# Filling the last block's gaps with the next gates, and re-ordering the entry of layer 3, in a four-layer graph network kernel

## The chip, the cores and the metric

The kernel runs on one core of one Trainium2 chip. The metric is device time in microseconds (us), the median of several runs; the profile comes from one further execution. The core's engines are named as in the profile: PE (matrix multiply), PEld (its weight loads), DVE (vector), ACT (scalar/activation), POOL (GpSimd) and SP (which here only issues DMAs). Each engine works through its own list of instructions in order and waits for others by semaphores.

## The reference, cut to what matters

Sixteen graphs (B) of 1024 nodes (N) with 256 features (D) pass through four pre-normalised layers. Each layer computes `h = relu(layernorm(x))` and adds its result to `x`. Layers 2 and 3 matter here:

```
# layer 2: a scan over nodes; node i reads rows that earlier nodes have already changed
norm_adjT = swapaxes(adj, 1, 2) / rowsum
def step(h, i):
    x = h_e[:, i];  x_par = norm_adjT[:, i] @ h
    r, z = sigmoid(split(x @ W_ioux.T + b_ioux + x_par @ W_iouh.T + b_iouh))
    hc = tanh(x @ W_coux.T + b_coux + (x_par * r) @ W_couh.T + b_couh)
    h[:, i] = z * x_par + (1 - z) * hc
# layer 3
agg = epsilon * h + adj @ h
y = silu(rmsnorm(agg @ W1 + b1)) ;  out = y @ W2 + b2
```

## The kernel before, in words

**Layers 0 and 1** come first and are not touched.

**Layer 2** cuts the 1024 nodes into NT = 8 blocks of 128 (`for t in range(NT)`) and each block into NS = 8 sub-slices of 16 nodes (`for s in range(NS)`), all sixteen graphs side by side. A sub-slice is computed in one or more steps (`SLICES`: one step of 16 nodes for s = 0 and 1, two of 8 for s = 2 to 6, and 8, 4, 4 with one repeated round for s = 7). A step is a chain across engines: `round_` multiplies by the recurrent weights (L1102, into `pr`, `pz`, `pc`), ACT applies sigmoid and tanh (L1146, L1153, L1163), DVE combines (L1147 to L1165), `turned` transposes the result (L1174) and ACT copies it out (L1177). Between two steps `x_change` (L1130) applies what the first step changed. At the end of a sub-slice PE computes `near`, the contribution to the next sub-slice (L1355), and DVE forms the next `x` from it (L1280).

A list `todo` holds independent PE work: contributions to later sub-slices (`far_tasks`, L1084, DVE adds them at L1087) and, while another block follows, the base sums of that next block (`base_tasks`, L935). `fill(weight)` takes pieces from `todo` and puts them between the steps of the chain; what a piece leaves to evict is queued in `late` and emitted by `evict()` at fixed places. The order of the instructions of PE, DVE, ACT and POOL in layer 2 is that of the program text.

The input side of the gates of the next sub-slice (`Gates`; three products of eight matmul records each, L1048, evicted by ACT for q = 0 at L1056 and by DVE for q = 1, 2 at L1053) is not in `todo`, except at s = 0. It is put in the two arms of a run-time branch (L1332): if a chain of dependent nodes is longer than the planned steps, `one_more` runs an extra round with the gates in its gaps; otherwise the Else arm runs the three gates one after the other. In the profiled execution the Else arm is what runs.

In the last block (t = 7) there is no next block, so `todo` holds only the far pieces. `early_3`, a generator, prepares layer 3 for graph 0 there: its first `next` issues the loads of `x`, of two adjacency quarters and of the layer-2 results; later calls normalise seven of the eight row tiles. For a tile DVE adds (L1413), takes statistics (L1415, L1416); then POOL takes the inverse root (L86) and ACT writes the relu (L1427). The kernel before calls it once per sub-slice, just ahead of the branch: three tiles per call, then the root and two diagonals, then all seven relus at once. Tile 7 exists only when layer 2 has ended and is done by `prepare(0)` in layer 3.

**Layer 3** works graph by graph. `sums` multiplies adjacency quarters by differences of `h` (a Strassen-like scheme of seven quarter products, L1522); the quarters go through six buffers `at`, filled by `fill(k)` (L1469), and five of the seven get epsilon added to their diagonals by POOL (`eps_of`, `diagonal`, L1389). `inner` multiplies by combinations of W1 (`ws`, L1568), `norm` and `outer` follow (L1639). At the entry POOL forms combinations of the weights (`ws` L1680 to L1683, `wt` L1687 to L1690), `row()` adds b2 to x (L1499), and `load(1)`, `prepare(1)` bring up graph 1. Only POOL follows the program text in layer 3; the order on the other engines, SP's issues among them, is made by a planner that also looks at costs and at the waits it is told (`issue_after`).

Entry order of POOL in the kernel before: root of tile 7, four `ws`, four `wt`, four pieces of `row`, then the diagonals of quarters 3, 4, 5, then that of quarter 6. SP: W1, tile 7's rows (`hn[0]` L1439), W2, b1, rms weight, b2, quarters 4 and 5, then x and the layer-2 rows of graph 1, then quarter 6.

Of the kernel before, what the change touches and what calls it, by code (L numbers as in the profile page):

```python
# [16 lines left out]
P = 128  # L17
# [25 lines left out]
def gnn_stack(ctx: ExitStack, tc: tile.TileContext, a: dict, out: bass.AP):  # L43
# [815 lines left out]
    def layer_2(shared, early):  # L859
        with ExitStack() as st:  # L860
# [172 lines left out]
            class Gates:  # L1033
# [9 lines left out]

                def gate(self, q):
                    pg = psum.tile([P, DC, G2 * GR], F32, name="pf", bufs=3)
                    for e in range(DC):
                        for c in range(DC):
                            nc.tensor.matmul(pg[:, e], wx[:, c, q * D + e * P : q * D + (e + 1) * P], self.hs[:, c],  # L1048
                                             start=c == 0, stop=c == DC - 1)

                    def out():
                        if q:
                            nc.vector.tensor_add(self.g[:, q], pg, bias[:, q][:, :, None].to_broadcast([P, DC, G2 * GR]))  # L1053
                        else:
                            for e in range(DC):
                                nc.scalar.activation(self.g[:, q, e], pg[:, e], AF.Identity, bias=bias[:, q, e : e + 1])  # L1056
                    return out
# [143 lines left out]
            with tc.manual_schedule(engines={mybir.EngineType.PE, mybir.EngineType.DVE, mybir.EngineType.Activation, mybir.EngineType.Pool}):  # L1201
# [19 lines left out]
                for t in range(NT):  # L1221
                    if t == NT - 1:
                        eye = next(early)
                    base_todo = deque()
                    if t + 1 < NT:
# [6 lines left out]
                    for s in range(NS):  # L1232
# [30 lines left out]
                        total = sum(cost for cost, _ in todo)  # L1263
                        spent = part = 0.0

                        def fill(weight):
                            nonlocal spent, part
                            part += weight
                            while todo and (part > 0.999 or spent + 0.5 * todo[0][0] < part * total):
                                cost, task = todo.pop(0)  # L1270
                                spent += cost
                                late.append(task() or (lambda: None))
# [22 lines left out]
                        for k, (i0, i1) in enumerate(steps):  # L1295
# [19 lines left out]
                            if k == 0:  # L1315
                                gx_now, gx = gx, gx_next
                                if s > 0 and sub_next:
                                    nc.gpsimd.tensor_copy(tick, rx[:, DC - 1].rearrange("p b i -> p (b i)")[:, :1] if K > 1
                                                          else rx[:, DC - 1, :1])
                                    gx = Gates(he if ahead[0] == t else he_next, ahead[1])  # L1320
                                    gx_ahead = Gates(he_next, 1) if s + 1 == NS else None
                            dh = h if last else work.tile([P, G2, D], F32, name="dh", bufs=1)
                            turned(change if twice else hT, rest_if(last, 0.5), dh)
                            if k == 0 and sub_next:
# [3 lines left out]
                                sub_next.own()  # L1328
                        if t == NT - 1 and s > 0:
                            next(early, None)  # L1330
                        in_arms = gx.tasks if gx and s > 0 else ()
                        with tc.If(n_more[0][s] > 0, preferred_fallthrough_block=False) as more_or_not:  # L1332
# [4 lines left out]
                        if in_arms:  # L1337
                            with more_or_not.Else():
                                for task in in_arms:
                                    late.append(task())  # L1340
                                    if len(late) > 1:
                                        late.pop(0)()
                                evict()
                        if gx:
                            gx.seed_r()
# [45 lines left out]
    def early_3(shared, pool, x, hn, at, h):  # L1391
# [20 lines left out]
        for t in range(n):  # L1412
# [3 lines left out]
            nc.vector.bn_aggr(mv[:, t], st)  # L1416
            if t % 3 == 2:
                yield
        rs = inv_sqrt(pool, mv[:, :, 1], LN_EPS, [P, n], "rs")
# [6 lines left out]
        for t in range(n):  # L1426
            nc.scalar.activation(h[0][:, t], x[0][:, t], AF.Relu, bias=shift[:, t : t + 1], scale=rs[:, t : t + 1])  # L1427
        yield

    def layer_3(shared, x, hn, at, h, eye):  # L1430
        with ExitStack() as st:
# [6 lines left out]
            eye, eye2 = eye  # L1438
            nc.sync.dma_start(hn[0][:, NT - 1], hs_d[NT - 1][0][:P])  # L1439
            w1 = wp.tile([P, DC, H], F32, name="w1")  # L1440
            nc.sync.dma_start(w1, a["W1"].rearrange("(c p) e -> p c e", p=P))
            w2 = wp.tile([P, HC, D], F32, name="w2")
            nc.sync.dma_start(w2, a["W2"].rearrange("(c p) e -> p c e", p=P))
            b1 = wp.tile([P, HC], F32, name="b1")
            rw = wp.tile([P, HC], F32, name="rw")
            with nc.allow_non_contiguous_dma(reason="weights, once"):
                nc.sync.dma_start(b1, a["b1"].rearrange("(c p) -> p c", p=P))
                nc.sync.dma_start(rw, a["rms_weight"].rearrange("(c p) -> p c", p=P))
            b2 = wp.tile([P, D], F32, name="b2")
            nc.sync.dma_start(b2, bcast_row(a["b2"], D))  # L1450

            NH = 512
            HH = HC // 2

            def load(b):
                if b:
                    x[b] = big.tile([P, NT, D], F32, name="x", bufs=3)
                    nc.sync.dma_start(x[b], rows(x2_d[b]))
                    hn[b] = shared.tile([P, NT, D], F32, name="hb")
                    nc.sync.dma_start(hn[b][:, : NT - 1], rows(hn_d[b])[:, : NT - 1])  # L1460
                    nc.sync.dma_start(hn[b][:, NT - 1], hs_d[NT - 1][b // GB][b % GB * P : (b % GB + 1) * P])

            NQ = len(ORDER)
# [10 lines left out]

            def prepare(b):

# [15 lines left out]
                nc.vector.scalar_tensor_tensor(shift, mv[:, part, 0], -1.0, rs, op0=ALU.mult, op1=ALU.mult)  # L1492
                for k, t in enumerate(tiles):
                    nc.scalar.activation(h[b][:, t], x[b][:, t], AF.Relu, bias=shift[:, k : k + 1], scale=rs[:, k : k + 1])  # L1494

# [15 lines left out]
            def sums(b, st, s4):  # L1511
# [29 lines left out]
                def third():  # L1541
# [9 lines left out]
                    product("s4", "b22", p7)  # L1551
                    nc.scalar.copy(tt[:, 2], p7)
                    nc.vector.tensor_sub(tt[:, 1], c11, p7)
                    nc.vector.tensor_sub(tt[:, 0], c22, tt[:, 1])
                    nc.vector.tensor_sub(tt[:, 3], c21, tt[:, 1])
                return (ag, tt), [first, second, third]

# [115 lines left out]

            load(0)
            for k in range(2, 6):
                fill(k)
            row = prepare(0)
            ws = wp.tile([P, 3, HH * P], F32, name="ws")
# [11 lines left out]
            nc.gpsimd.tensor_tensor(wt[:, 2], v21, wt[:, 1], ALU.subtract)  # L1690
            row()
            load(1)
            for k in range(2, 6):
                eps_of(k)
            st3, steps3 = differences(0)
            for step3 in steps3[:3]:
                step3()
            ags, parts = sums(0, st3, steps3[3])
            parts[0]()
            eps_of(NQ - 1)  # L1700
            parts[1]()
            parts[2]()
            prepare(1)()
            for k in range(4):
                eps_of(NQ + k)
            for b in range(B):
# [11 lines left out]
                if b + 1 < B:  # L1718
                    ags, parts = sums(b + 1, st3, s4)
                parts[0]()  # L1720
# [77 lines left out]
```

## Time and profile before

| | us |
|---|---|
| median of 3 runs | 4227.49 (4225.37 to 4234.3) |
| profiled execution, its own time | 4226.12 |
| its span, first to last instruction | 4224.4 |
| one block of layer 2, from near of s = 1 to the next block's (blocks 0 to 5) | about 202 |
| last block, near of s = 1 (2794.84) to the first product of layer 3 (2959.10) | 164.3 |
| first product of layer 3 to the first product of `inner` that follows the sums (3008.70) | 49.6 |
| one graph of layer 3, in the steady part | 76.2 |

Over the whole span PE is busy 95%, DVE 62%, ACT 39%, POOL 39%, and the granted clock of TensorE is 0.985. These are averages: a row of stretches (start and end in us, then busy us and instruction count of each engine, the granted clock as a share of full speed, the busy share of the DMA engines and GB/s) tells more. In the timeline rows the columns are start, duration (of a merged group), engine, line, operation, tiles, count, and in brackets the idle time before it and who ended it. Matmul records of one group overlap slightly in time; a gate product of four matmuls shows as eight records.

### The profile page before, as it was taken

To read this page: it belongs to the slowest core of one execution; us is meant where nothing else is said; L and a number is where in the kernel's file an instruction comes from. 1 tells how busy PE (TensorE), PEld (TensorE's weight loads), DVE (VectorE), ACT (ScalarE), POOL (GpSimd) and SP (SyncE) were. 2 spreads that over 40 slices of the span, in tenths; PEclk is the share of its full clock that TensorE was granted. 3 is DMA by queue.
4 is the path that set the end of the run, shared out by engine and by line. 5 is a ranking of instruction groups with operands and counts; after the bars stand their busy time and mean duration, and the time that the engine had idled before them with its cause. 6 is when DMAs were issued, how large, how long until landed. Compare 5 with 4: busy or idle time off the path is not lost. (4 is left out here: it accounts for less than half of the span.)

```text
span 4224.4 us, 56649 instructions
## 1 busy us (share of the span) xinstructions
PE 4018.3 (95%) x19307; PEld 2802.1 (66%) x19307; DVE 2614.6 (62%) x6218; ACT 1635.4 (39%) x4172; POOL 1646.5 (39%) x1740
## 2 busy tenths in 40 slices
PE   7999999998997999999999999998899999999998
PEld 3545455555555888888888888877365665756656
DVE  7888976577762444444444444453577877777776
ACT  3565565544543232232323232323233334333332
POOL 2232223434334324333333333332546355464552
PEclk9999999999998999999999999998899999999999
DMA  7576657988768454645464554421633434334320
GB/s 244 207 238 232 230 200 261 265 301 285 262 212 269 135 197 135 200 136 186 153 193 145 189 163 162 155 99 36 214 120 137 163 120 146 134 121 174 114 100 21
DMA packets 406704, 744.74 MB, mean 176 GB/s; under 512 B 75168, under 2 KB 325664, under 8 KB 365344
## 3 DMA queue, kind: packets, MB, share of 16 engines
q1 hardware_dynamic: 370976, 613.49, 42.5%
q0 software_dynamic: 26080, 109.21, 9.0%
q10 hardware_dynamic: 9216, 16.78, 1.1%
q8 instruction: 210, 3.44, 0.3%
q14 instruction: 222, 1.82, 0.1%
HBM read 538.85 MB, written 183.76 MB: 171 GB/s over the span
## 5 line engine op out<-in xcount | busy, mean ns | idle before, releaser
L86 POOL TENSOR_TENSOR rs<-rs_v,mhalf 128x8 f32<-128x8 f32 (+1 forms) x65 | 112.3, 1728 | 900.4 <-DVE rs_v L82 469.7
L935 PE MATMUL pf<-hb,ab 128*128 128x256 f32 x1568 | 415.2, 383 | 0.0
L1048 PE MATMUL pf<-hs,wx 128*128 128x256 f32 x1536 | 347.7, 383 | 13.0 <-POOL hs L1039 12.7
L1048 PEld LDWEIGHTS pf<-hs,wx 128*128 128x128 f32 x1536 | 293.5, 192 | 56.2 <-POOL hs L1039 13.8
L1348 POOL DMA_INDIRECT hs_d<-h,table x128 | 129.3, 1010 | 464.6 <-ACT gates L1056 404.3
L1576 POOL TENSOR_TENSOR ss<-ss,sq 128x512 f32<-128x512 f32 x224 | 299.2, 1351 | 23.8 <-ACT sq L1574 17.8
L935 PEld LDWEIGHTS pf<-hb,ab 128*128 128x128 f32 x1568 | 272.1, 191 | 37.3 <-issue 6.7
L1053 DVE TENSOR_TENSOR gates<-pf,bias 128x512 f32<-128x512 f32 x128 | 88.5, 692 | 288.3 <-PE pf L1048 248.4
L423 PE MATMUL pmm<-w,ag 128*128 128x256 f32 x1024 | 234.6, 387 | 20.4 <-DVE x L427 8.8
L1639 PEld LDWEIGHTS po<-w,hh 128*128 128x128 f32 x2048 | 237.9, 193 | 16.6 <-issue 11.0
L1639 PE MATMUL po<-w,hh 128*128 128x128 f32 x2048 | 242.1, 277 | 1.4 <-ACT hh L1622 0.7
L423 PEld LDWEIGHTS pmm<-w,ag 128*128 128x128 f32 x1024 | 196.1, 194 | 61.6 <-DVE x L427 12.6
L1574 ACT ACTIVATE sq<-hh 128x512 f32<-128x512 f32 x224 | 141.6, 632 | 197.7 <-POOL ss L1576 118.7
L1522 PE MATMUL ph<-bxt,hb 128*128 128x512 f32 x440 | 198.9, 598 | 4.1 <-ACT hb L1494 2.6
L1146 ACT ACTIVATE r<-pr 128x128 f32<-128x128 f32 (+2 forms) x256 | 57.9, 278 | 366.4 <-PE pr L1102 306.4
L1084 PE MATMUL pf<-bd,h 128*128 128x384 f32 (+4 forms) x512 | 185.1, 451 | 0.8 <-DVE bxt L1087 0.8
L1087 DVE TENSOR_TENSOR bxt<-bxt,pf 128x384 f32<-128x384 f32 (+4 forms) x256 | 128.0, 501 | 82.3 <-PE pf L1084 79.5
L1572 DVE SCALAR_TENSOR_TENSOR hh<-ph,b,u 128x512 f32<-128x512 f32 x192 | 141.5, 749 | 47.0 <-PE ph L1568 36.9
L1622 ACT ACTIVATE hh<-hh,rw 128x512 f32<-128x512 f32 x256 | 158.9, 711 | 24.1 <-DVE hh L1621 24.1
L345 ACT ACTIVATE pt<-x,m_neg 128x256 f32<-128x256 f32 x240 | 114.5, 477 | 109.0 <-DVE m_neg L340 102.7
L1621 DVE TENSOR_TENSOR hh<-hh,po 128x512 f32<-128x512 f32 x256 | 154.3, 679 | 2.9 <-PE po L1618 2.9
L1494 ACT ACTIVATE hb<-x,shift,rs 128x256 f32<-128x256 f32 x120 | 60.9, 591 | 239.6 <-DVE shift L1492 239.6
(371 smaller groups left out, 9283.3 us busy)
## 6 DMA issues: line engine op xcount, KB each, us to landing
at<-in_quarters SPq DMA_DIRECT2D x94, 1024.0 KB
t_d<-at SPq DMA_DIRECT2D x64, 1024.0 KB
ab<-in_columns SPq DMA_DIRECT2D x127, 512.0 KB
bxt<-t_d SPq DMA_DIRECT2D x42, 1024.0 KB
bxt<-in_quarters SPq DMA_DIRECT2D x34, 1024.0 KB
at<-at POOLq DMA_DIRECT2D x30, 1024.0 KB, 7.1
at<-t_d SPq DMA_DIRECT2D x22, 1024.0 KB
pc<-in_own ACTq DMA_DIRECT2D x64, 256.0 KB
```

The source lines that it names most:

```text
L423: nc.tensor.matmul(po[:, t - t0], ag[:, c, t * P : (t + 1) * P], w[:, c], start=c == 0, stop=c == DC - 1)
L935: nc.tensor.matmul(pb, ab[:, jts[k]], hb[:, jts[k]], start=k == 0, stop=k == len(jts) - 1)
L1048: nc.tensor.matmul(pg[:, e], wx[:, c, q * D + e * P : q * D + (e + 1) * P], self.hs[:, c], start=c == 0, stop=c == DC - 1)
L1084: nc.tensor.matmul(pf, h[:, g, c * P : (c + 1) * P], bd[:, g, b0 : b0 + n, S : S + far], start=True, stop=True)
L1348: nc.gpsimd.indirect_dma_start(out=hs_d[t][g][:, :], out_offset=row(1, g, t, s), in_=h[:, g], in_offset=None)
L1522: nc.tensor.matmul(pa, st[left][:, k], at[q % 6][:, k], start=onto is None and k == 0, stop=k == 3, skip_group_check=True)
L1572: behind3[:] = [nc.vector.scalar_tensor_tensor(hh[q][:, k], ph, b1[:, k : k + 1], u, op0=ALU.add, op1=ALU.add)]
L1574: nc.scalar.activation(sq, hh[q][:, k], AF.Square)
L1576: nc.gpsimd.tensor_tensor(ss[q], ss[q], sq, ALU.add)
L1621: nc.vector.tensor_mul(hh[q][:, k], hh[q][:, k], pr)
L1622: nc.scalar.activation(hh[q][:, k], hh[q][:, k], AF.Silu, scale=rw[:, k : k + 1])
L1639: nc.tensor.matmul(po[:, n], left[:, c, n * P : (n + 1) * P], right[:, c], start=onto is None and n == 0 and c == 0, stop=c == HH - 1, ski ...
```

## The change

Four things are done.

1. In the last block, for s = 1 to 6, two of the three next gates are appended to `todo` once `x` of the next sub-slice's gates can be read, so that `fill` places them between the steps; one stays in the arms. In every block the last gate's PSUM tile is now taken ahead of the branch, and its eviction is emitted after the branch (`out_of_arms`) and not in both arms.
2. `early_3` yields after every tile, in the statistics and in the relus, and is called from `fill` (so from `late`) for s > 1 in the last block, in place of one call per sub-slice for s > 0.
3. At the entry of layer 3 the fills and diagonals of quarters 2 to 5 come ahead of the weights, b2 ahead of W2, tile 7's rows behind W2; `row()` of graph 0 and `load(1)` come ahead of the `ws`/`wt` combinations on POOL.
4. The relus of graph 1 (`prepare(1)`) are told to be issued after the ACT copy `tt` at the end of graph 0's sums.

```diff
-                def gate(self, q):
-                    pg = psum.tile([P, DC, G2 * GR], F32, name="pf", bufs=3)
+                def gate(self, q, pg=None):
+                    if pg is None:
+                        pg = psum.tile([P, DC, G2 * GR], F32, name="pf", bufs=3)
...
-                    base_todo = deque()
+                    base_todo = None
...
+                        in_arms, out_of_arms = [], None
                         def fill(weight):
                             nonlocal spent, part
+                            if t == NT - 1 and s > 1:
+                                late.append(lambda: next(early, None))
                             part += weight
...
                                     gx = Gates(he if ahead[0] == t else he_next, ahead[1])
                                     gx_ahead = Gates(he_next, 1) if s + 1 == NS else None
+                                    n = 0 if base_todo is not None else 2
+                                    todo += [(1.72, task) for task in gx.tasks[:n]]
+                                    total += 1.72 * n
+                                    in_arms = gx.tasks[n:]
...
-                        if t == NT - 1 and s > 0:
-                            next(early, None)
-                        in_arms = gx.tasks if gx and s > 0 else ()
+                        if in_arms:
+                            pg = psum.tile([P, DC, G2 * GR], F32, name="pf", bufs=3)
+                            def last_gate():
+                                nonlocal out_of_arms
+                                out_of_arms = gx.gate(2, pg)
+                                return lambda: None
+                            in_arms = in_arms[:-1] + [last_gate]
                         with tc.If(n_more[0][s] > 0, ...) as more_or_not:
...
+                            out_of_arms()
                         if gx:
                             gx.seed_r()
...
             nc.vector.bn_aggr(mv[:, t], st)
-            if t % 3 == 2:
-                yield
+            yield
...
             nc.scalar.activation(h[0][:, t], x[0][:, t], AF.Relu, ...)
-        yield
+            yield
...
     def layer_3(shared, x, hn, at, h, eye):
...
-            nc.sync.dma_start(hn[0][:, NT - 1], hs_d[NT - 1][0][:P])
+            for k in range(2, 6):
+                fill(k)
+                eps_of(k)
             w1 = ...load W1
+            b2 = ...load b2
             w2 = ...load W2
+            nc.sync.dma_start(hn[0][:, NT - 1], hs_d[NT - 1][0][:P])
             b1, rw = ...load b1, rms_weight
-            b2 = ...load b2
...
-            def prepare(b):
+            def prepare(b, behind=None):
...
+                with tc.issue_after(behind) if behind is not None else ExitStack():
                     for k, t in enumerate(tiles):
                         nc.scalar.activation(h[b][:, t], ...)
...
-                    nc.scalar.copy(tt[:, 2], p7)
+                    got["tt"] = nc.scalar.copy(tt[:, 2], p7)
...
-            load(0)
-            for k in range(2, 6):
-                fill(k)
-            row = prepare(0)
+            prepare(0)()
+            load(1)
             ws = ...four POOL operations; wt = ...four POOL operations
-            row()
-            load(1)
-            for k in range(2, 6):
-                eps_of(k)
...
-            prepare(1)()
+            prepare(1, got["tt"].ins)()
```

In the instruction lists as built, SP now issues at the entry: W1, quarters 4 and 5, b2, W2, tile 7's rows, b1, rms weight, quarter 6, then x and the layer-2 rows of graph 1. POOL has the diagonal of quarter 3 inside sub-slice 7 of the last block, and at the entry the diagonals of quarters 4 and 5, the root of tile 7, `row`, `ws`, `wt`, the diagonal of quarter 6. In the last block's sub-slices 2 to 6 one gate stands between `x_change` and the second step's `pc` (behind `x_change` for s = 3 to 6, behind `pz` for s = 2), the other between that `pc` and the transposes. For graph 0, DVE's additions and statistics of graph 1 stand ahead of the first `u` (L1544), and ACT has the eight relus of graph 1 behind `tt` and ahead of `inner`'s first copy `p` (L1584).

## The prediction

> **What bounds the kernel now.** First the share of each engine, then the busy time by stretch, cut at the start of each `near` product in the last block and at the two ends of layer 3's entry. In the base blocks PE is full; the stretches that the change touches are those where it isn't.
>
> ```profile
> 2794.80:2814.80 20.00, 17.36 (x76) 13.30 (x77) 14.57 (x31) 4.50 (x11) 13.24 (x18) 1.00 0.10 32
> 2814.80:2835.60 20.80, 19.14 (x112) 15.03 (x113) 13.35 (x39) 6.46 (x20) 7.73 (x12) 1.00 0.06 20
> 2855.70:2879.10 23.40, 20.67 (x105) 16.68 (x105) 9.30 (x27) 9.65 (x27) 7.37 (x14) 0.85 0.07 19
> 2900.90:2920.40 19.50, 16.18 (x104) 13.77 (x105) 8.03 (x26) 6.46 (x20) 6.05 (x10) 1.00 0.08 24
> 2920.40:2959.10 38.70, 29.82 (x144) 26.52 (x144) 10.21 (x41) 8.38 (x34) 0.22 (x2) 0.61 0.16 58
> 2959.10:3008.70 49.60, 29.81 (x59) 12.00 (x59) 18.04 (x37) 4.70 (x9) 26.73 (x21) 0.84 0.81 292
> ```
>
> Sub-slice 6 (fourth row) has PE idle 3.3 of 19.5 us; sub-slice 4 (third) also lost clock, 0.85 granted; the entry of layer 3 (last) has PE idle 20 of 49.6. Then PE's timeline of sub-slice 4 and of the entry.
>
> ```profile
> 2862.42 0.87 PE L1174 MATMUL pa<-ident,hT 128*128 128x128 f32 x4 [1.25 <-DVE hT L1165]
> 2864.15 1.94 PE L1130 MATMUL pa<-ai,dh 128*128 128x64 f32 x8 [0.85 <-ACT dh L1177]
> 2873.58 5.38 PE L1048 MATMUL pf<-hs,wx 128*128 128x256 f32 x24
> ...
> 2970.78 1.12 PE L1522 MATMUL ph<-bxt,hb 128*128 128x512 f32 x2 [2.60 <-ACT hb L1494]
> 2972.01 3.70 PE L1522 MATMUL ph<-bxt,d 128*128 128x512 f32 x8
> 2986.68 5.42 PE L1522 MATMUL ph<-bxt,d 128*128 128x512 f32 x8 [10.97 <-POOL bxt L1389]
> 3008.70 2.08 PE L1568 MATMUL ph<-tt,ws 128*128 128x512 f32 x2 [5.43 <-DVE tt L1553]
> ```
>
> The three gates run in one piece (5.38) while gaps of about a microsecond stay empty. At the entry PE waits 10.97 for the diagonal of quarter 3, which stands on POOL behind twelve operations, and 5.43 for `tt`, whose copy on ACT stands behind two relus of graph 1. POOL's and SP's own rows there:
>
> ```profile
> 2980.49 4.91 POOL L1499 TENSOR_TENSOR x<-hb,b 128x512 f32<-128x512 f32 x4
> 2985.37 1.26 POOL L1389 TENSOR_TENSOR bxt<-bxt,eye 128x512 f32<-128x512 f32 x1
> 2964.79 0.32 SPq L1439 DMA_DIRECT2D hb<-hs_d  x1
> 2998.00:3000.00 2.00, 2.00 (x6) 0.90 (x5) 1.18 (x4) 0.13 (x1) 0.00 (x0) 1.00 1.01 422
> ```
>
> **The gates.** One gate is 5.38/3 = 1.79 us of PE. Moving two takes 3.59 off each arm, six times: 21.5. What they cost in the gaps: in sub-slice 6 (19.55 long, times from its start) `x_change` starts at 7.72 and the next `pr` at 9.18. A gate starting at 8.64 pushes `pr` to 10.37, +1.2. The far pieces once there go into the 0.85 gap ahead of `x_change`: two of 0.39, free. The second gate runs from 13.15 to 14.95, where the shifted transposes would start at 14.5: +0.45. Net -1.95. For sub-slice 5 the same sum gives 18.2 instead of 21.8 (far pieces 1.17 for a gap of 0.85, +0.2), because its rows at 1.74 (x_change), 1.61 (pr) are slowed by clock and should not be. For sub-slice 4, 18.5 instead of 23.4.
>
> [...] The trace's clock drops at 2863.89 though PE's longest idle piece just before is 1.25; the slow records (1.94 for an L1130 group that takes 1.08 elsewhere) last 6.8 us. [...] By the row, scattered gaps do it, and filling the 0.85 one and shortening others regains up to 3.3 more, -4.9. I take -4.0, nearer the row.
>
> Each gate needs `hs`, copied by POOL behind two scatters and two gathers (about 1.3 us each) that start when the sub-slice's result is out: some 5.6 after `near`'s start, against a gate at 8.6. In sub-slice 3 the root and two diagonals go first on POOL (1.52 + 2.48) and `hs` comes at about 9.6, just in time: 0 to 1 us, I take 0.1.
>
> **The rows of layer 3.** In the kernel before, three tiles and two epsilon tiles on DVE (about 5.7) stand ahead of gate evictions in sub-slice 1, and `near` waits 1.83 for them: -1.8. In sub-slice 2 DVE gets, between its chain work, seven tiles of 0.39 + 0.43 + 0.18 = 1.0 and two small tiles, while its chain operations stand behind: +1.2 at the first `r`, +0.1 at the transposes, +2.2 where `x_change` waits for PSUM tiles that DVE has still to clear (two tiles ahead of the evictions), +1.2 at the second `pc` with the gate, +0.3 at the end: about +4.9, less 3.6 of the arm and 0.4 for the two groups no longer ahead of `near`: +0.9. If DVE's tiles fall wholly into its idle (20.8 - 13.35 = 7.45 us), -2.5; if each tile is on the chain, +4. Sub-slice 3 gets the seven relus of 0.5 on ACT: +0.3 ahead of `r`, +0.3 ahead of the second tanh, and far pieces of 1.02 ahead of `x_change`, +1.1; with the gates +0.2: -1.7. Sum of the last block: -1.8 + 0.9 - 1.7 - 4.0 - 3.6 - 1.95 = -12.2. Sub-slice 7 has no gate and stays.
>
> **All blocks.** The last gate's eviction (0.69 on DVE) moves behind the branch; DVE waits for PE's last gate there as before. `near` waits for PE's own count, unchanged. The rotating PSUM tile taken first is now the last to be cleared; the next piece that wants it comes a `near` (1.13) and mostly a `pnx` (1.06) later, and the eviction ends about 0.9 after `near` starts, so it is hidden, except where a block ends (only 1.05 cover): some 0.1 us times 7, +0.6. Without that cover it would be up to 0.7 at each of 49 boundaries.
>
> **The entry.** Diagonals 4 and 5 now wait for their quarters; diagonal 3 falls into sub-slice 7, where POOL is idle. So PE's 10.97 goes. What is late next: tile 7's rows stand on SP's queue behind 4.2 MB (W1, two quarters, b2, W2) instead of W1 alone. By the row, 2964.79 issued to DVE's start at 2966.80, they land in 2.0 us. [...] This case's rates are 0.31 MB/us for W1 with the scatters (2960 to 2964) and 0.42 at best (row above): 2959.6 + 1.3/0.31 + 3.4/0.42 = 2972. [...]
>
> From there: pair 1.2; `d` products 5.5 at a cold clock (PE has idled 7.8, and after its 10.97 idle the same form took 5.42) and 3.6, then 7.0 and 3.5 for the last: the sums end at 2996.7; POOL is in time (root 2974.1, row to 2979, `ws` to 2984.9, `wt` to 2990.8, diagonal 6 to 2992.1, wanted at 2993.2). `load(1)` goes out at 2979, when `row` frees the buffer (2985.4 before), lands by 2983.5; DVE's statistics of graph 1 (6.2) end by 2991. `tt` follows the sums at once: PE starts at 2998.4 instead of 3008.70. ACT then has eight relus (4.1) ahead of `p`, which frees the first PSUM tile at 3002.2; PE has five, of 0.86 each, so it stalls as if the first product had started at 2997.9, against 3007.84 before: -9.9. If tile 7's rows land as before, -15; if at half the rate (2984), +1.
>
> Fills for graph 1 (6 MB at 0.42, 15 us from 2983) are wanted from about 3028. The steady part, 76.2 per graph, has the same work, so the shift reaches the end.
>
> **Sum.** -12.2 + 0.6 + 0.1 - 9.9 = -21.4 on the profiled 4226.1, which lies 1.4 under the median; on the median 4227.5 - 21.4 = 4206.1.
>
> **The rivals.** (a) The entry gives only 2 or so, tile 7's rows at 2980 (0.25 MB/us): for it, W1 moved at 0.31 and W2's short packets are no better; against it, 0.42 in the quarters. 4214. (b) The last block gives only 4: row tiles on the chain in sub-slice 2 (+4) and clock not regained in 4 and 5 (+5). [...] 4214. (c) The gaps regain more, the clock also in sub-slice 7 (0.61 granted over 38.7 us): 4196. Unforced, nothing there is filled. (d) Slower: PE waits at each of 49 boundaries for the last gate's eviction because of the PSUM rotation. From 0.44 us each it eats the gain; at the full 0.69 it is 34 us, so 4239. The timeline (eviction over at 2108.96, PE's first use at 2110.20) speaks against it. (e) The moved gates hide nothing, each pushing the chain by its whole 1.79: the last block nets +3, the entry -10: 4221, about no change.
>
> **How the numbers follow.** Main 0.60 (4199 to 4213), a 0.13, b 0.11, c 0.06, d 0.05, e 0.05. The range leaves out d, most of e and the far half of c: 4197 to 4220. What a measurement here tells from no change is 0.2%, 8.5 us. Faster (under 4219): main, c, nearly all of a and b: 0.85; same 0.10; slower 0.05.
>
> **What would show it.** Arms of eight L1049 records (1.8) in the last block; `near` distances of about 18, 22, 18, 18.5, 18, 17.5 from s = 1; blocks 0 to 5 still 202.0; clock 1.00 in sub-slice 4. At the entry: no POOL wait of 11 ahead of the second `d` product, tile 7's add on DVE some 5 us later than 7.7 after the first L1522, `tt` right behind the sums. Wrong if blocks lengthen, if sub-slice 2 grows by over 4, or if the entry (49.6) stays above 46.

## The result, and the profile after

The changed kernel takes 4209.52 us (median of 6 runs, 4201.68 to 4214.37), against 4228.32 (4225.35 to 4234.3) for the kernel before. The ratio is 0.9952, with an interval from 0.9941 to 0.9962: 20 us less by it, with an interval of 16 to 25 (the medians lie 18.8 apart). The forecast was 4206.1, with a range of 4197 to 4220.

The profiled execution of the changed kernel has a span of 4199.8, which is 24.6 under that of before. Of this, 3.8 are there already at the first `near` of layer 2, before anything that the change touches (1380.27 against 1384.05), and 0.5 come up in blocks 0 to 6. Such differences are those of one execution from another. What the change did is read from the last block's first `near` to the end: 1429.57 before, 1409.25 after, so 20.3 less. The stretches after, in the same columns as those of before:

```profile
2790.60:2808.80 18.20, 17.33 (x76) 13.24 (x77) 9.15 (x20) 4.51 (x11) 11.74 (x17) 1.00 0.09 26
2808.80:2830.10 21.30, 19.17 (x112) 14.99 (x113) 17.22 (x54) 6.46 (x20) 7.95 (x12) 1.00 0.07 22
...
2848.80:2866.50 17.70, 16.92 (x104) 13.94 (x104) 9.80 (x26) 6.46 (x20) 7.00 (x13) 1.00 0.08 25
...
2884.50:2901.90 17.40, 15.49 (x105) 13.71 (x105) 8.67 (x26) 6.47 (x20) 5.86 (x11) 1.00 0.09 26
2901.90:2940.20 38.30, 29.18 (x144) 26.13 (x144) 10.08 (x41) 8.38 (x34) 2.69 (x4) 0.62 0.17 63
2940.20:2984.30 44.10, 31.27 (x58) 12.64 (x58) 20.03 (x37) 3.12 (x6) 26.14 (x19) 0.78 0.85 299
```

Sub-slice 4 (third row) fell from 23.4 to 17.7, and its clock from 0.85 to 1.00. Sub-slice 7 (fifth row) is unchanged, at a clock of 0.62. The entry (last row) fell from 49.6 to 44.1 and not to about 39. PE's timeline shows where the three gates went and what the entry now waits for:

```profile
2857.79 1.95 PE L1049 MATMUL pf<-hs,wx 128*128 128x256 f32 x8
...
2862.37 1.89 PE L1049 MATMUL pf<-hs,wx 128*128 128x256 f32 x8
2864.10 0.60 PE L1175 MATMUL pa<-ident,hT 128*128 128x128 f32 x4
2864.53 1.89 PE L1049 MATMUL pf<-hs,wx 128*128 128x256 f32 x8
...
2960.63 2.08 PE L1538 MATMUL ph<-bxt,hb 128*128 128x512 f32 x2 [10.54 <-ACT hb L1510]
2962.50 8.81 PE L1538 MATMUL ph<-bxt,d 128*128 128x512 f32 x16
2971.14 7.03 PE L1538 MATMUL ph<-at,hb 128*128 128x512 f32 x16
2979.24 3.67 PE L1538 MATMUL ph<-bxt,hb 128*128 128x512 f32 x8 [1.07 <-POOL bxt L1403]
2984.31 1.12 PE L1584 MATMUL ph<-tt,ws 128*128 128x512 f32 x2 [0.54 <-DVE tt L1569]
```

The wait of 10.97 for POOL's diagonal is gone, and so are 4.9 of the 5.43 for `tt`. In their place the wait for tile 7's relu has grown from 2.60 to 10.54. Behind it stand tile 7's rows:

```profile
2940.45 1.00 POOL L1362 DMA_INDIRECT hs_d<-h,table  x1 [27.46 <-ACTq L1345]
...
2942.00 0.38 SPq L1474 DMA_DIRECT2D w<-in_W  x1
2947.66 0.75 SPq L1475 DMA_DIRECT2D hb<-hs_d  x1
...
2956.66 0.43 DVE L1499 TENSOR_TENSOR hb<-hb 128x256 f32<-128x256 f32 x1 [18.07 <-DMA hb<-hs_d]
```

SP issues them 7.4 after the first quarter product (2940.22), and DVE has them 9.0 later: 16.4 after that product, where before it was 7.7. The load reads what the first of the two last scatters writes (L1362; graphs 0 to 7), and SP issues it when that scatter has landed, 7.2 after POOL issued it. In the kernel before this took 5.5 (issue of the load at 2964.79):

```profile
2959.33 0.98 POOL L1348 DMA_INDIRECT hs_d<-h,table  x1 [37.96 <-ACTq L1332]
```

### The profile page after: what moved, and what is told of

Its sections match the earlier page's. It is cut to its first block, busy times and chain, and to the rows that moved or that the text cites. A ratio compares the mean times of both kernels' runs of the same rounds, so it can differ in the third digit from the quotient of the medians.

```text
span 4199.8 us, 56656 instructions
## 1 busy us (share of the span) xinstructions
PE 4008.7 (95%) x19307; PEld 2796.3 (67%) x19307; DVE 2614.5 (62%) x6218; ACT 1634.5 (39%) x4172; POOL 1648.1 (39%) x1740
## 5 line engine op out<-in xcount | busy, mean ns | idle before, releaser
L1362 POOL DMA_INDIRECT hs_d<-h,table x128 | 129.3, 1010 | 444.4 <-ACT gates L1057 366.4
L1588 DVE SCALAR_TENSOR_TENSOR hh<-ph,b,u 128x512 f32<-128x512 f32 x192 | 141.1, 749 | 43.9 <-PE ph L1584 34.1
L1538 PEld LDWEIGHTS ph<-bxt,hb 128*128 128x128 f32 x440 | 82.9, 193 | 111.3 <-issue 92.8
```

Of the source, the lines that this page charges most:

```text
L1362: nc.gpsimd.indirect_dma_start(out=hs_d[t][g][:, :], out_offset=row(1, g, t, s), in_=h[:, g], in_offset=None)
L1538: nc.tensor.matmul(pa, st[left][:, k], at[q % 6][:, k], start=onto is None and k == 0, stop=k == 3, skip_group_check=True)
L1588: behind3[:] = [nc.vector.scalar_tensor_tensor(hh[q][:, k], ph, b1[:, k : k + 1], u, op0=ALU.add, op1=ALU.add)]
```

## The experiments

A chip has runs of the kernel before beside each group of kernels. The medians scatter by several microseconds, so the stretches of the profiled execution decide between causes. "Entry" runs from the first quarter product to the first product of `inner` that follows the sums, "to the end" from the last block's first `near`. There is one trace of each kernel. How far a stretch moves without any change of its code can be read from the table: the entry of the changed kernel lies between 43.3 and 44.1 in the five kernels that have it as it is, that of before between 49.6 and 50.3 in three, and s = 7 without added work between 38.2 and 39.4.

| kernel | median us (before, same chip) | ratio, interval | sub-slices 1 to 6 | s = 7 | tile 7's add, from first quarter product | entry | to the end |
|---|---|---|---|---|---|---|---|
| before | | | 125.6 | 38.7 | +7.7 | 49.6 | 1429.6 |
| changed | 4209.5 (4228.3) | 0.9952, 0.9941 to 0.9962 | 111.3 | 38.3 | +16.4 | 44.1 | 1409.3 |
| l2_only | 4214.9 (4225.8) | 0.9977, 0.9968 to 0.9986 | 111.1 | 38.5 | +7.9 | 50.3 | 1415.7 |
| entry_only | 4218.8 (4225.8) | 0.9988, 0.9979 to 0.9997 | 124.5 | 38.5 | +15.8 | 43.4 | 1421.6 |
| row_ahead_w2 | 4201.4 (4225.8) | 0.9946, 0.9932 to 0.9959 | 111.1 | 39.4 | +11.6 | 39.3 | 1406.5 |
| row_act | 4201.1 (4225.8) | 0.9944, 0.9931 to 0.9958 | 111.1 | 38.7 | +15.0 | 41.7 | 1407.6 |
| row_first | 4202.8 (4224.4) | 0.9955, 0.9942 to 0.9968 | 111.1 | 39.1 | +7.8 | 40.4 | 1407.1 |
| row_root | 4209.9 (4227.5) | 0.9955, 0.994 to 0.997 | 111.3 | 38.5 | +7.8 | 43.7 | 1409.1 |
| no_behind | 4209.8 (4227.5) | 0.995, 0.9935 to 0.9965 | 111.3 | 39.3 | +16.4 | 47.0 | 1411.1 |
| no_gates | 4217.4 (4224.4) | 0.9983, 0.9974 to 0.9992 | 125.1 | 38.2 | +15.7 | 43.3 | 1422.5 |
| s4_warm_before | 4221.8 (4224.4) | 0.9997, 0.9987 to 1.0006 | 122.4 | 38.6 | +7.4 | 49.6 | 1426.2 |
| s7_warm | 4203.7 (4224.4) | 0.9954, 0.9941 to 0.9967 | 111.1 | 37.6 | +16.4 | 44.0 | 1407.6 |
| s7_hold | 4198.0 (4227.5) | 0.9922, 0.9908 to 0.9936 | 111.3 | 29.6 | +16.3 | 44.0 | 1401.4 |
| best2 | 4192.8 (4223.8) | 0.9933, 0.9919 to 0.9947 | 111.1 | 29.8 | +9.5 | 39.8 | 1396.3 |

**The two halves, each alone.** l2_only has the changed `layer_2` and `early_3` with the `layer_3` of before; entry_only is the reverse.

> Layer 2 of the changed kernel (two gates in the gaps, rows of layer 3 by tile) with the entry of layer 3 of the kernel before. Theory A (the two halves of the change are independent): the last block alone gives -14.3 +/- 1, so about 4214 against 4228.3, and the entry from the first quarter product to inner stays 49.6. Rival B (the lost part of the entry's forecast comes from layer 2, whose rows by tile or single gate leave the entry later): the entry here is already longer than 49.6 by 2 or more, and the total gives less than -12.

> Layer 2 of the kernel before, entry of layer 3 of the changed kernel. Theory A: the entry is 44.1 as in the changed kernel, so -5.5 and about 4222.8; the sum of this run's gain and that of the layer-2-only kernel is the whole gain of -20. Rival B (layer 2's new end delays the entry): the entry here reaches the forecast of about 39.7, so -9.9 and 4218.4.

Alone, layer 2 gives 13.8 to the end and the entry 8.0; together they should give 21.8, and the change gives 20.3. So the halves are nearly independent (theory A), and the entry falls short by itself: 43.4, not 39.7. (entry_only's median is close to rival B's 4218.4, but before is 2.5 faster on that chip than beside the changed kernel; the entry decides.) The 1.1 that entry_only has in sub-slices 1 to 6, in which its code is that of before, show how much one execution's clock can move: half-clock stretches fell on 2882 to 2889 and 2906 to 2909 here, so that sub-slice 4 took 20.1 and sub-slice 5 22.7, against 23.4 and 21.8 in the profile of before.

**The gates without the rest, and filler in place of gates.** no_gates leaves all three gates in the arms; s4_warm_before adds to the kernel before products that nothing reads.

```diff
-                                    n = 0 if base_todo is not None else 2
+                                    n = 0                                   # no_gates
```

```diff
+    # s4_warm_before: in s = 3, 4, 5 of the last block, behind every pc and behind every set of transposes
+    spare = psum.tile([P, DC, G2 * GR], F32, name="pf", bufs=3)
+    nc.tensor.matmul(spare[:, 0], ident, wx[:, 0, :256], start=True, stop=True)
```

> The changed kernel with all three gates of the last block left in the arms, the rows of layer 3 still by tile. Theory A (the gates give most of s = 3 to 6): distances near 18.2, 21, 20.5, 21 to 23, 21, 19.5, so the last block 122 to 125 against 111.3, half-clock windows back in s = 4 or 5, and s = 1 keeps its gain of 1.8. Rival F (the rows by tile give most): 112 to 117.

> The kernel before with added work that nothing reads: in s = 3, 4, 5 of the last block one product of 128x256 (0.45 of PE) behind every pc and one behind every set of transposes, 1.8 per sub-slice. Theory A (scattered gaps of about a microsecond cost the clock, and filling them keeps it): no half-clock windows between 2830 and 2900, and the three distances together, 65.2 in the kernel before, are no longer or even shorter (61 to 65) in spite of 5.4 of added work. Rival E (the clock falls for another reason, the gates' gain is only the work taken from the arms): half-clock windows stay and the three grow by 2 to 5, to 67 to 70.

Stretches of sub-slices 3 to 5, first s4_warm_before, then no_gates:

```profile
2829.83:2850.30 20.47, 19.89 (x113) 15.35 (x113) 10.96 (x30) 6.46 (x20) 9.74 (x14) 1.00 0.05 16
2850.30:2870.62 20.32, 19.30 (x113) 15.25 (x113) 9.54 (x27) 9.76 (x27) 7.53 (x13) 1.00 0.07 22
2870.62:2890.62 20.00, 18.70 (x113) 15.19 (x113) 8.79 (x26) 6.46 (x20) 8.21 (x14) 1.00 0.09 30
```

```profile
2837.14:2857.01 19.87, 18.29 (x104) 13.88 (x105) 9.92 (x27) 9.75 (x27) 9.13 (x14) 1.00 0.09 30
2857.01:2878.13 21.12, 19.12 (x104) 15.13 (x105) 9.21 (x26) 6.46 (x20) 7.19 (x13) 0.92 0.07 21
2878.13:2899.15 21.02, 18.43 (x104) 15.36 (x105) 8.68 (x26) 6.46 (x20) 6.76 (x12) 0.92 0.07 21
```

With 5.4 of added work the three sub-slices are shorter than before, 60.8 against 65.2, at full clock. Part of the 4.4 is where the half-clock stretches fall: one of 3.4 us moved to the edge of sub-slice 6 (20.9 there, 19.6 before). Over sub-slices 1 to 6 it is 3.2 less with the work than without, and 2.1 less than in entry_only, which has the same layer 2 without the work. So filling small gaps does buy clock, as the three clocks of 1.00 show; the medians do not tell s4_warm_before from the kernel before (0.9987 to 1.0006). no_gates gives 125.1: all but 0.5 of the last block's gain comes from the gates, and the rows by tile only moved time from sub-slice 1 (18.2, 1.7 less) into sub-slice 2 (22.5, 1.7 more). Rival F falls.

**What the clock follows.** In all 14 traces the clock is either full or half and changes only on a grid of 3.41 us. I counted for each such window the columns that PE's matmul records moved (an f32 product has two records, so one of 512 counts 1,024; a record counts where it starts), and looked at the clock in the next window:

| columns in a window | windows | next window at half clock |
|---|---|---|
| under 1,280 | 365 | 364 |
| 1,280 to 1,535 | 59 | 52 |
| 1,536 to 1,791 | 160 | 46 |
| 1,792 to 2,047 | 188 | 9 |
| 2,048 and more | 16,293 | 2 |

(How the idle ends of a trace are taken moves the first row by some 30 windows, the middle rows by 5 or less.) In the traces of the kernel before and of the changed one the commonest count is 4,096 at full clock (937 of 2,385 windows) and 2,048 at half clock (16 of 70). Parted by the clock of the counted window itself, the limits lie close together but not at one place: of the windows at full clock, 210 of 216 under 1,536 columns were followed by half clock and 19 of 16,454 with more; of those at half clock, 263 of 269 under 1,664 were followed by half clock again and 10 of 219 with more. So in these traces, but for the windows named, full clock was kept from some 38% of its commonest count on (1,536 of 4,096), while from half clock PE came back only from some 80% on (1,664 of 2,048).

Two simpler rivals sort the same windows worse. With the best single cut for each, columns misplace 23 of the 16,670 windows at full clock, the busy share of PE 70 and its longest gap 75; of the 488 at half clock they misplace 15, 59 and 73. In s = 7 of the changed kernel a window at half clock has about 800 columns (320 to 1,024). Two kernels add products of 128x256 that nothing reads there: s7_warm has two behind every `pc` and one behind every set of transposes, s7_hold two behind each of these and one behind every `x_change`. s7_warm was made for the theory of gaps, s7_hold for that of columns, when the table held only the runs before it.

> The changed kernel with added work that nothing reads in s = 7 of the last block: two products of 128x256 behind every pc and one behind every set of transposes (1.35 of PE per step, four steps). Theory A (gaps cost the clock, half of full for 34 us here): no half-clock window in s = 7, which falls from 38.3 to 27 to 31, and the first quarter product of layer 3 runs at full clock: 8 to 12 less in all. Rival E (clock falls for another reason, or the added work stands in the way of the chain): s = 7 stays at 38 or grows up to 42.

> The changed kernel with more added work in s = 7 of the last block that nothing reads: products of 128x256, two behind every pc, two behind every set of transposes, one behind every x_change, so that a window of 3.41 us holds more than about 1,640 moved columns (the count that parts windows followed by full clock from those followed by half clock in the traces so far; 820 in s = 7 of the changed kernel, 1,210 to 1,660 with three such products per step). Theory G (the clock follows the columns moved in the window before, not the length of gaps): no or nearly no half-clock window in s = 7, which falls from 38.3 to 28 to 31; the first quarter products run at full clock; 7 to 10 less in all. Rival E (the clock in s = 7 is halved for another reason): half clock stays and s = 7 grows to 39 to 45.

The stretch of s = 7, first in s7_warm, then in s7_hold:

```profile
2900.21:2937.81 37.60, 34.41 (x169) 29.04 (x169) 10.33 (x41) 8.37 (x34) 3.17 (x5) 0.70 0.17 64
```

```profile
2906.05:2935.62 29.57, 27.48 (x182) 22.55 (x183) 10.23 (x41) 8.37 (x34) 3.26 (x5) 1.00 0.21 81
```

s7_warm missed its forecast: PE is busy 34.4 of 37.6, hardly a gap is left, and the clock is still halved for most of it. That was what turned the question from gaps to columns: products of 64 columns are short, and its windows hold 860 to 1,790. With 1,980 to 3,200 in s7_hold the clock stays full, and s = 7 takes 29.6 instead of 38.3 with 7 more products in it than s7_warm. Theory G's forecast of 28 to 31 holds; s7_hold is faster than the changed kernel by 7.9 to the end, and the intervals of their ratios do not meet.

**Where tile 7's rows go.** Four kernels move the load; only the last of them, row_root, changes POOL's order too.

```diff
# row_ahead_w2: behind quarters 4, 5 and ahead of b2 and W2; row_act: the same place, nc.scalar instead of nc.sync
             w1 = ...load W1
+            nc.sync.dma_start(hn[0][:, NT - 1], hs_d[NT - 1][0][:P])
             b2 = ...load b2
             w2 = ...load W2
-            nc.sync.dma_start(hn[0][:, NT - 1], hs_d[NT - 1][0][:P])
```

> The changed kernel with tile 7's rows put ahead of b2 and W2 in SP's queue (1.1 MB less ahead of them; SP then waits for the last scatter before it issues W2). Theory A (the rows are late because of the bytes ahead of them in their own queue): DVE's add of tile 7 starts about 12 after the first quarter product (16.4 in the changed kernel) and the entry shortens from 44.1 by 3 to 6: about 4204 to 4207 against 4209.5. Rival C (the rows are late because of the wait for the last scatter and the time of a transfer, not of the queue): add at 15 or later, entry 43 or more, and W2, issued some 5 later, makes POOL's combinations late. Rival D (another wait takes the place): add early, entry unchanged.

> The changed kernel with tile 7's rows brought by ACT's DMA queue instead of SP's, so that nothing stands ahead of them in their queue and W2 doesn't wait for the scatter. Theory A: add of tile 7 at 9 to 11 after the first quarter product, entry 37 to 40, about 4203 to 4205. Rival C (engine sharing: the packets take turns with the 4 MB of SP's queue, so the queue makes no difference): add at 14 or later and the entry above 42.

row_act's answer is the telling one. From the timelines of ACT and of DVE in it:

```profile
2954.14 0.58 ACT L1549 COPY p<-ph 128x512 f32<-128x512 f32 x1 [8.03 <-DMA hs_d<-h,table]
...
2961.17 0.42 DVE L1499 TENSOR_TENSOR hb<-hb 128x256 f32<-128x256 f32 x1 [16.59 <-DMA hb<-hs_d]
```

With a queue of its own the load goes out as soon as its scatter has landed (issue at 2953.62, 7.2 after POOL issued the scatter) and still takes 7.5. The DMA packets of the trace show when: its first piece of 1 KB moves 4.4 after the issue, its last 7.0 after it, and all that time SP's queue moves the quarters, b2 and W2, at the end also 4-byte pieces. Rival C holds for the add (15.0, where it named 14 or later): being alone in a queue brings it forward by only 1.5 (the entry, 41.7, is just under the 42 that it named). ACT's copy `p` waits 8.03 behind the issue and PE 2.79 for that copy (0.68 in the changed kernel); PE then waits 7.51 for tile 7's relu, so that this is hidden. In row_ahead_w2 the same load takes 4.1, with the quarters ahead and b2 and W2 held back behind it. Its entry, 39.3, is 4.8 shorter, as theory A forecast. What W2 and what the small pieces cost was not tested apart.

row_first puts the load right behind W1, ahead of quarters 4 and 5, as it was before the change. row_root then also turns POOL's order.

```diff
# row_first: the load of tile 7's rows now stands ahead of the fills in the text; SP issues W1, rows, quarters 4, 5, b2, W2
+            nc.sync.dma_start(hn[0][:, NT - 1], hs_d[NT - 1][0][:P])
             for k in range(2, 6):
                 fill(k)
+            for k in range(2, 4):          # row_root only
                 eps_of(k)
...
             w2 = ...load W2
-            nc.sync.dma_start(hn[0][:, NT - 1], hs_d[NT - 1][0][:P])
...
             prepare(0)()
+            for k in range(4, 6):          # row_root only
+                eps_of(k)
             load(1)
```

> The changed kernel with tile 7's rows issued right behind W1 and ahead of quarters 4 and 5, b2 and W2, as in the kernel before; all else of the entry stays. Theory A (what delays the rows is all that moves beside the last scatter and beside the rows themselves, both 7 us each in the changed kernel, 5.5 and 2.0 before): add of tile 7 at about +8 after the first quarter product, entry 34 to 37, time from the last block's first near to the end 7 to 10 below the changed kernel's 1409.3. Rival D (quarters 4 and 5 or W2, issued some 5 later, become the wait): add at +8, but the entry stays at 39 or more, no better than with the rows ahead of W2 (39.3).

> The kernel with tile 7's rows right behind W1, and on POOL the root of tile 7 and row ahead of the diagonals of quarters 4 and 5, which stood ahead of them and waited for their quarters until 14 after the first quarter product. Theory A: add at +8, first product that needs tile 7's relu at +11.5 to +12.5 (17.7 with the diagonals ahead, 20.4 in the changed kernel); the entry 36 to 39, since then the last diagonal, behind ws and wt on POOL (+34 to +36), is next to be waited for. Rival D (quarters 4 and 5 come too late, or POOL's row is): entry 40 or more.

Now the scatter lands 5.6 after its issue (5.7 in row_root) and the load takes 2.0, as in the kernel before: DVE adds at +7.8. (The 7 that row_first's expectation gives for the load in the changed kernel is 9.0.) But row_first's entry is 40.4 and not 34 to 37, so that rival D's forecast came true. POOL's timeline shows why:

```profile
2955.10 1.26 POOL L1403 TENSOR_TENSOR at<-at,eye 128x512 f32<-128x512 f32 x1 [8.79 <-DMA at<-t_d]
2957.73 1.26 POOL L1403 TENSOR_TENSOR at<-at,eye 128x512 f32<-128x512 f32 x1 [1.37 <-DMA at<-t_d]
2958.95 0.58 POOL L86 TENSOR_TENSOR rs<-rs_v,mhalf 128x1 f32<-128x1 f32 x1
```

The two diagonals, ahead of the root of tile 7 in POOL's order, wait for their quarters, and the root waits with them: 6 of the 8.6 won are lost there. In row_root the root goes first, and PE takes the pair that needs it at +10.7. Then, on PE's timeline, three waits take its place:

```profile
2954.68 1.12 PE L1539 MATMUL ph<-bxt,hb 128*128 128x512 f32 x2 [1.10 <-ACT hb L1511]
2955.64 7.03 PE L1539 MATMUL ph<-bxt,d 128*128 128x512 f32 x16
2967.01 9.97 PE L1539 MATMUL ph<-at,hb 128*128 128x512 f32 x16 [4.33 <-POOL at L1403]
...
2979.92 3.70 PE L1539 MATMUL ph<-bxt,hb 128*128 128x512 f32 x8 [2.09 <-POOL bxt L1403]
2987.65 2.07 PE L1585 MATMUL ph<-tt,ws 128*128 128x512 f32 x2 [4.02 <-DVE tt L1570]
```

POOL's `row`, now ahead of the diagonals, started only at 2960.81, 7.0 after the root; b2, which it reads, stands behind two quarters in SP's queue. That b2 was what it waited for is inferred from that order. Rival D holds: entry 43.7. The wait for `tt` is DVE's: graph 1's statistics stand ahead of it and begin only at 2977.62, behind DVE's work for the sums; their rows are loaded only when `row` has freed the buffer (issue at 2965.76). Which of the two makes them late was not tested apart.

**The fourth part.** no_behind drops the wait of graph 1's relus for `tt`.

```diff
-            prepare(1, got["tt"].ins)()
+            prepare(1)()
```

> The changed kernel without its fourth part: the eight relus of graph 1 aren't told to wait for ACT's copy tt. Theory A: the relus come as soon as graph 1's statistics are out, by then the sums are nearly over, so that at most two of them (0.5 each) stand ahead of tt: entry 44 to 46, within 2 of the changed kernel. Rival H (this part was what removed the 5.4 us wait for tt): entry 47 to 49.

The entry grows by 2.9, to 47.0, between the two forecasts. PE's timeline parts it:

```profile
2989.77 5.37 PE L1538 MATMUL ph<-bxt,hb 128*128 128x512 f32 x8 [2.30 <-issue]
...
2997.78 1.12 PE L1584 MATMUL ph<-tt,ws 128*128 128x512 f32 x2 [1.79 <-DVE tt L1569]
```

All eight relus (4.0), not two, went ahead of `tt`, and the wait for it grew from 0.54 to 1.79. The rest, 1.7, is the last quarter product, which took 5.37 here against 3.67; four of its eight records at half clock (0.86 and not 0.43 each, an estimate from the products of `inner` in the kernel before, 1.91 and 1.02 for two) would give that. `inner` then runs without its stall (74.7 from its first `tt` product to graph 1's first product, 76.4 in the changed kernel). To the end the trace shows 1.8 more, of which 1.0 lies in s = 7, whose code is the same, so that this part is not shown to be worth anything.

**Both findings together.** best2 has the added products of s7_hold, b2 ahead of W1, the rows behind W1, the root and `row` ahead of the diagonals, the last diagonal ahead of `wt`, and the rms weights later.

> The changed kernel with both findings together: the added work of the kernel with five products per step in s = 7, and an entry in which b2 comes ahead of W1, tile 7's rows right behind W1, and on POOL the root of tile 7 and row ahead of the diagonals of quarters 4 and 5, the last diagonal ahead of wt, the rms weights' load behind graph 0's sums. Theory: s = 7 at 29.6; add of tile 7 at +8, the pair that needs tile 7 at +11, diagonals at +16 to +18, ws at +23, last diagonal at +25, so the sums run through to +30 and the entry is 32 to 36 (44.1 in the changed kernel); time about 4209.5 - 8.5 - 10 = 4191, range 4187 to 4197. Rival D (quarters 4 and 5, or graph 1's rows and their statistics on DVE ahead of tt, become the wait, as in the last try): entry 40 or more, 4198 or more.

It takes 4192.8, ratio 0.9933 (0.9919 to 0.9947): under both kernels, and 13.0 under the changed one to the end. The median lies in the forecast range by luck: before is 4.5 faster on this chip than beside the changed kernel, and the entry missed its 32 to 36. At 39.8 it is no better than row_ahead_w2's, as rival D had it. PE's timeline in best2 names the rest:

```profile
2946.81 2.08 PE L1547 MATMUL ph<-bxt,hb 128*128 128x512 f32 x2 [6.24 <-ACT hb L1519]
...
2973.18 2.07 PE L1593 MATMUL ph<-tt,ws 128*128 128x512 f32 x2 [5.16 <-DVE tt L1578]
```

The rows arrive at +9.5, their scatter having taken 7.9 with b2 and W1 in flight (5.6 in row_first, with W1 alone), and the statistics of graph 1 stand ahead of `tt` on DVE again. An order with these behind `tt` was not tried.

## Why the prediction was right, and where it was not

The forecast of 21.4 less met 20.3 in the trace, and that is partly luck, for errors cancelled: sub-slices 1 to 6 gave 2.1 more, the entry 4.2 less, and 0.7 of small costs did not show.

**Last block, sub-slices 1 to 6, -12.2 forecast, -14.3 measured.** By sub-slice: -1.8, +0.9, -1.7, -4.0, -3.6, -1.95 were forecast; -1.73, +0.47, -1.35, -5.66, -3.85, -2.15 came. That the gates fill the gaps was right. So was the sum of sub-slices 1 and 2, where the rows by tile fall (-0.9 forecast, -1.26 measured; in no_gates these rows change nothing on balance). The mis-sized term is sub-slice 4. The forecast took -4.0 for it, 0.9 less than the -4.9 that it read off the row; that reserve was the author's estimate, and no run shows it. The row was right and even short: -5.66. Where the clock is full, the kernel of before takes 20.1 for sub-slice 4 (entry_only), so 3.3 were clock, all that the row promised, and 2.4 the gates, where 1.6 was reckoned. Long gaps were not needed for half clock: in s = 7 of the changed kernel no gap is longer than 1.5, and 34.1 us from 2911.5 on, 28.7 of them in s = 7, run at half clock. But the "why" of the row, scattered gaps, was only half of it: s7_warm filled the gaps and kept the half clock.

**All blocks, +0.6 forecast, nothing measured.** Blocks 0 to 4 differ by at most 0.11 each. The eviction behind the branch is hidden at block ends too; rival (d) is out.

**Sub-slice 7, unchanged as forecast** (38.68 and 38.34). Rival (c), full clock there, came only with 2,560 more columns in each step but one (s7_hold).

**The entry, -9.9 forecast, -5.7 measured**, 5.5 of it in the entry and 0.2 behind it. The removed waits and the place of `tt` were right. The step that failed is the arrival of tile 7's rows, "2959.6 + 1.3/0.31 + 3.4/0.42 = 2972", 12.9 after the first quarter product; it was 16.4. Of this sum the term 3.4/0.42 is mis-sized, and in it the part that is not quarters. Up to the end of the quarters it held: W1 and the quarters, pieces of 4 and 8 KB, moved about at the rates assumed (1.05 MB of W1 in 3.7, then 0.39 to 0.44 MB/us from 2944 to 2948, the scatters included), and the first piece of 1 KB started 9.3 after the first quarter product, where the sum gives 9.7. Behind it b2, W2 and the rows, 1,280 pieces of 1 KB or 1.31 MB, took 6.6 where 0.42 MB/us gives 3.1. The rows of the changed kernel show it (the last column is GB/s, the first quarter product is at 2940.2):

```profile
2946.00:2948.00 2.00, 1.32 (x4) 0.49 (x3) 0.00 (x0) 0.59 (x1) 0.00 (x0) 1.00 1.05 436
2948.00:2950.00 2.00, 2.00 (x5) 0.57 (x3) 0.00 (x0) 0.00 (x0) 0.76 (x1) 1.00 0.97 364
2950.00:2952.00 2.00, 0.09 (x1) 0.00 (x0) 0.00 (x0) 0.00 (x0) 1.05 (x2) 1.00 0.84 188
2952.00:2954.00 2.00, 0.00 (x0) 0.00 (x0) 0.00 (x0) 0.00 (x0) 0.71 (x1) 0.60 1.09 355
2954.00:2956.00 2.00, 0.00 (x0) 0.00 (x0) 0.00 (x0) 0.00 (x0) 0.00 (x0) 0.50 0.75 88
```

By the packets of the trace the first 256 of these pieces (b2 and the beginning of W2) took 2.0, the next 896 took 2.7, and the last 128, beside most of the 2,048 pieces of 4 bytes of b1 and the rms weights, 1.9. These 4-byte pieces were not in the sum at all. Why the first 256 are slow is open. The wait for the scatter is not what made the rows late here: it ended at +7.4, with the quarters ahead still moving until +10.7. Rival (a) had named this mechanism, short packets that are slow, and was put aside for the 0.42 of the quarters; its size, an entry that gives only 2, was too large. row_ahead_w2 shows the size: 4.8 of entry back for moving one load.

The sum of that step takes the rows as arriving behind all 4.2 MB issued ahead of them in their queue, and the forecast's sums end at 2996.7 because PE's wait for their relu was put 4.0 behind the arrival, at 2976.0. That the rows must come last was assumed, and no run shows it for them alone. What the packets of the changed kernel show fits it: the 8 KB pieces of the quarters start between +3.6 and +10.3 of the first quarter product, the pieces of 1 KB, those of the rows among them, between +9.3 and +15.8. The 4.0 came true (add at 2956.66, PE at 2960.63). But row_act, 1.5 better with a queue of its own, shows that the place in the queue was the smaller part. The second term that failed is "POOL is in time": PE waits 1.07 for the last diagonal, which stands on POOL behind the late root and behind a `row` that took 5.8 and not 4.9.

## What to carry to other kernels

Here a transfer that was needed soon was delayed by what was in flight, before it in its queue or in another one (128 KB took 9.0 and 7.5 from issue to use, against 2.0 with little else in flight): hold large and small-piece loads back until it is out (4.1 in row_ahead_w2), reckon small pieces at a rate of their own (0.20 MB/us here, against 0.39 to 0.44), and then look at what stands behind it on each in-order engine, for in row_first two diagonals that waited for late quarters held up a root that was ready, and cost 6 of the 8.6 won. Read the clock by the columns that PE moves in each clock window (3.41 us here), not by how long it idles: in s7_warm a chain of narrow products was half-clocked almost without a gap (PE busy 34.4 of 37.6, mean clock 0.70). Useful wide work from elsewhere (here the next gates) or, failing that, useless work can be worth more than its own length, but only if there is enough of it: 12 added products gave 0.7, 19 gave 8.7. A forecast that came true in sum should still be checked by stretch.

## What the runs showed of the hardware

- The clock of a 3.41 us window went with the columns moved in the window before: 364 of 365 windows under 1,280 were followed by half clock, 16,291 of 16,293 with 2,048 or more by full.
- Work that nothing reads made the program faster: 19 added products, 8.7 less in s = 7 (29.6 against 38.3).
- Of the windows at half clock, 263 of 269 under 1,664 columns (some 80% of their commonest count, 2,048) were followed by half clock again, and 10 of 219 with more.
- 128 KB took 2.0 from issue to use with little else in flight (before, row_first), 7.5 in a queue of its own beside 1 MB in pieces of 1 KB and 8 KB in pieces of 4 bytes (row_act), and 9.0 in one queue with these, behind the megabyte (changed kernel).
- 1.31 MB in pieces of 1 KB, with 4-byte pieces among the last, moved at 0.20 MB/us in the changed kernel, where the traffic just before, mostly pieces of 8 KB, moved at 0.39 to 0.44 (2944 to 2948).
- A scatter of 128 rows landed 5.5 after its issue beside W1 alone, 7.2 with two quarters behind W1, and 7.9 beside b2 and W1 (before, changed kernel, best2). An SP issue of b1 or the rms weights, 4 KB in pieces of 4 bytes, took 0.4 to 6.0.
